# A selective-scan network on one core: the 3x3 convolution in 15 products of up to 128 rows, and the sums of chunks 0 and 1 copied out later

## The chip, the cores and the metric

The kernel runs on one core of a Trainium2 chip. The core has four compute engines, each with its own queue of instructions that it takes in order: TensorE (PE in the profile; its weight loads are PEld), VectorE (DVE), ScalarE (ACT) and GpSimd (POOL). SyncE (SP) issues the DMAs that this kernel uses, also in order. The metric is the device time of one execution in microseconds; smaller is better. Three runs of the kernel before took 5869.17, 5872.94 and 5878.88 us, so the median is 5872.94 us.

## The reference

The input is four images of 64 x 64 positions and 96 channels. Layer 0, which the change concerns, is group norm, then this (cut):

```python
xz = x @ W_in.T                      # 96 -> 384
xp, z = xz[..., :192], xz[..., 192:]
xc = silu(conv3x3(xp, conv_w) + conv_b)          # 192 -> 192 channels, zero padding
# four scans of 4096 positions: rows, columns, and both reversed
dts, Bs, Cs = split(x_proj_w @ xs)               # 6, 16 and 16 rows
delta = softplus(dt_proj_w @ dts + dt_proj_b)
h = exp(delta * A) * h + (delta * u) * B         # 16 states for each of 192 channels
y = sum(h * C, over states) + D * u
out = (sum of the four y) * silu(z) @ W_out.T
```

After it come a depthwise and a pointwise convolution with batch norm, linear attention with a feed-forward layer in 8-bit floats, and a filter by FFT over the 4096 positions with another such feed-forward layer.

## The kernel before, in words

**The head.** Image 0 goes through `before_scans` alone, ahead of all scans: `project` (load x, normalise, multiply with `w_in` to the 192 convolution inputs), `project_z`, `convolve`, `gates` and `scan_inputs`. An image is 8 blocks of 8 rows (512 positions). For each block and each half of 96 output channels, `convolve` adds up 18 products, 9 taps by 2 halves of 96 input channels. Its input `xp` has no padding, so a tap that would reach over the edge of the image writes a smaller window of the output (504, 448 or 441 columns in place of 512). Images 1 to 3 go through the same code beside the scans.

**The scans.** There are N = 192 phases: image, row or column order, and one of 24 groups of 8 channels; 8 channels by 16 states make 128 partitions. A phase has 4 chunks of 1024 positions. First come four forward steps, q = 0 to 3, then four reverse steps, k = 0 to 3 over chunks 3 to 0. This order is written by hand for all engines:

- ACT: `decay` (line 1458) writes exp(delta x A) of a chunk to PSUM (`pa`). The decays of chunks 1 and 0 are made a second time for the reverse steps, by `decay(n, 1, False)` at k = 1 and `decay(n, 0, True)` at k = 2; the next phase's first, `decay(n + 1, 0, True)`, is made at k = 3.
- DVE: the scan of a chunk (line 1700 forward, 1749 reverse), and the addition of the reverse scan to the forward one (line 1759). Once the convolutions are all done, chunk 0's reverse scan stays apart in its delta tile instead (`apart`), which spares that addition and costs POOL and PE one more operation each.
- POOL: `times_b` (line 1441) ahead of the scans, and `times_c` (1445, and `times_c_apart`, 1450) after them.
- PE: `reduce` (line 1472) adds the states up with a matrix of ones, in two halves of a phase (chunks 0 and 1, chunks 2 and 3), into one PSUM bank `py`. ACT copies it out (`result`, line 1480), and SP stores it in four DMAs (`store_result`, line 1489).
- SP: `load_delta` and `load_du` (both by way of line 1413) fetch a chunk for later phases, two DMAs each. Delta tiles have 5 buffers, `dl0` to `dl4`, which `place_of` gives out.

**Work beside the scans.** After each forward or reverse step, `pieces` puts in a piece of other work (images 1 to 3 up to their scans, turning of rows to columns, later layers of finished images), as far as each engine's credit goes: each piece names its cost by engine in `yield (PE, ACT, POOL, DVE, DMA)`, and a table gives credit by step. So costs in the code decide where a piece stands in the queues.

**The tail.** After the last phase, image 3 goes through the remaining layers alone.

Of the kernel before, what the change touches and what calls it, by code (L numbers as in the profile page):

```python
# [10 lines left out]
F32 = mybir.dt.float32  # L11
# [8 lines left out]
HW = 64  # L20
# [53 lines left out]
def layers(ctx: ExitStack, tc: tile.TileContext, a: dict, out):  # L74
# [110 lines left out]
    us, xps, xbs, szs = {}, {}, {}, {}  # L185
# [84 lines left out]
    def before_scans(b, wk, take, deep=1, prev=None):  # L270
# [3 lines left out]
        _, w_in, conv_w, xproj, dt_w = kept  # L274

        def count(stage):

            before = NBLK if prev is None else done[stage, prev]
            return done.get((stage, b), 0) + before - NBLK

        def project():
# [14 lines left out]
            for i in range(NBLK):  # L296
# [11 lines left out]
                xp = xps[b, i] = wk.tile([C, 2, RPB + 2, HW], F32, tag="xp", name="xp", bufs=2)  # L308
                for c in range(2):
                    for ra, rb in ((0, 5), (5, n)):  # L310
                        p, give = yield from take("p_xp", C, (rb - ra) * HW)
                        yield (0.8, 0, 0, 0)
                        nc.tensor.matmul(
                            p, lhsT=w_in[:, c * C : (c + 1) * C], rhs=xb[:, ra:rb, :],
                            start=True, stop=True,
                        )
                        yield NEXT
                        yield (0, 0.42, 0, 0)
                        nc.scalar.copy(xp[:, c, ra:rb, :], p.rearrange("p (r w) -> p r w", w=HW))
                        give()  # L320
# [26 lines left out]
        def convolve():  # L347
            for i in range(NBLK):
                yield from until(lambda: i < count("project"))
                r0, lo, hi = rows_of(i)  # L350
                xp = xps.pop((b, i))
                for oc in range(2):
                    p, give = yield from take("p_conv")
                    pr = p.rearrange("p (r w) -> p r w", w=HW)
                    todo = [(t, kc) for t in conv_taps() for kc in range(2)]
                    for k, ((ky, kx), kc) in enumerate(todo):
                        if k % 3 == 0:
                            yield (2.4, 0, 0, 0)
                        dy, dx, ra, rb, ca_, cb_ = tap_window(ky, kx, r0)
                        at = r0 + dy - lo  # L360
                        nc.tensor.matmul(  # L361
                            pr[:, ra:rb, ca_:cb_],
                            lhsT=conv_w[:, kc, ky * 3 + kx, oc * C : (oc + 1) * C],
                            rhs=xp[:, kc, at + ra : at + rb, ca_ + dx : cb_ + dx],
                            start=(k == 0), stop=(k == len(todo) - 1),
                        )
# [1002 lines left out]
    def last_place(name, k):  # L1369

        if (name, k) not in last_tiles:
            tags = {
                "w_in": [f"B{4 * (N % 2) + q}" for q in range(4)],
                "sz_in": [f"dl{place_of(*x)}" for x in ((N - 1, 3), (N - 1, 2), (N - 1, 1), (N, 0))],
# [30 lines left out]

    def channel_halves(t):

        return [t[k * 64 : k * 64 + 64, :] for k in range(2)]
# [6 lines left out]
    def load_delta(n, q):  # L1415
        if n < N:
            b, g, o = phases[n]
            t = dls[n, q] = big.tile([128, CH], F32, tag=f"dl{place_of(n, q)}", name="dl")
            load_channels(t, delta_s[o][b], g, q)
# [194 lines left out]
    for _ in group_norm(start.sbuf("start"), take, (0,), lambda: True):  # L1614
        pass
    start.close()
    kept += [
        const("w_in", [C, 2 * DI], a["w_inT"], wk),
        const("conv_w", [C, 2, 9, DI], a["convT"], wk),
# [47 lines left out]
    with tc.manual_schedule():  # L1667
        ordered[0] = True
        pas = [decay(0, 0, True), None, None, None]
        for n in range(N + 1):  # L1670
# [3 lines left out]
            for q in range(NCH):  # L1674
# [3 lines left out]
                else:  # L1678
                    load_delta(n + 1, 4 - q)
# [12 lines left out]
                else:  # L1692
                    times_b(n + 1, 0)
                    reduce(n - 1, 0, (0,))
# [12 lines left out]
            if end:  # L1707
                result(n - 1, 0)
# [13 lines left out]
            for k, q in enumerate(reversed(range(NCH))):  # L1722
# [4 lines left out]
                if k == 0:  # L1727
                    result(n - 1, 0)
                    load_delta(n + 1, 0)
                elif k == 1:  # L1730
                    store_result(n - 1, 0)
                    load_du(n + 2, 0)
                elif k == 2:
                    load_delta(n + 1, 3)
                else:
                    load_du(n + 2, 1)
# [4 lines left out]
                elif k == 2:  # L1741
                    pas[0] = decay(n, 0, True)
                elif k == 3:
# [43 lines left out]
def host_layout(i):  # L1787
# [7 lines left out]
    o["convT"] = f(w.transpose(2, 1, 3, 0))  # L1795
# [92 lines left out]
```

## Time and profile before

| | |
|---|---|
| median of three runs | 5872.94 us |
| profiled execution, its own time | 5867.99 us |
| its span | 5866.2 us |
| PE busy | 4369.5 us (74%) |
| DVE busy | 4801.4 us (82%) |
| ACT busy | 3018.7 us (51%) |
| POOL busy | 4413.7 us (75%) |
| moved by DMA | 1173 MB, 200 GB/s on average |
| granted TensorE clock, mean | 0.778 |

A line of the groups view names the line of the kernel, the engine, the operation, what it writes and reads with their shapes, and the count; behind the first bar stands busy time and the mean duration in ns, and behind the second the engine's idle time just before these instructions and what ended most of it. A line of the waits view reads "who waited <- for whom: us in total, times, longest". An fp32 product leaves two records in the trace. The record count of line 361, 2304, is so twice the 1152 products of the convolution.

### The profile page before, as it was taken

The numbers are of one execution on the slowest core, as the hardware profiler recorded it, in microseconds if no ns is written. First come the engines' busy times: TensorE is split into PE (matmuls) and PEld (weight loads), VectorE is DVE, ScalarE is ACT, GpSimd is POOL, SyncE is SP. The second block draws the span as 40 slices with busy tenths as digits, with TensorE's granted clock in tenths as the row PEclk, the third lists the DMA queues.
The fourth block names the chain that finished last, engine by engine and source line by source line (L and its number), as shares of the span: only waits on it lengthen the run. The fifth ranks groups of instructions, "written<-read, shape, count | busy, mean of one in ns | idle before, by whom it ended". The sixth has DMA issues, their size and how long they took to land. (4 is left out here: it accounts for less than half of the span.)

```text
span 5866.2 us, 64908 instructions
## 1 busy us (share of the span) xinstructions
PE 4369.5 (74%) x20038; PEld 1680.1 (29%) x20038; DVE 4801.4 (82%) x3479; ACT 3018.7 (51%) x4141; POOL 4413.7 (75%) x2118
## 2 busy tenths in 40 slices
PE   8978898799884776664566776667678667667888
PEld 3322222222220221142331221245222114333345
DVE  2049889889889888999889999999988999979364
ACT  4557666676555346645444546434444554424233
POOL 0258888789879778988778989888897898867200
PEclk9979889899886776666777876668678766767888
DMA  3258868887679878788988867679987578886003
GB/s 100 77 155 237 233 200 229 224 233 214 199 218 246 226 201 224 208 247 239 251 234 227 227 178 214 191 211 251 233 230 205 164 210 233 242 230 194 23 37 105
DMA packets 469417, 1173.13 MB, mean 200 GB/s; under 512 B 90496, under 2 KB 155628, under 8 KB 468972
## 3 DMA queue, kind: packets, MB, share of 16 engines
q1 hardware_dynamic: 469068, 1168.97, 72.5%
q8 instruction: 159, 2.61, 0.2%
q14 instruction: 190, 1.56, 0.1%
HBM read 1011.86 MB, written 156.76 MB: 199 GB/s over the span
## 5 line engine op out<-in xcount | busy, mean ns | idle before, releaser
L1445 POOL TENSOR_TENSOR S<-S,rep 128x1024 f32<-128x1024 f32 x768 | 1807.9, 2356 | 580.6 <-DVE S L1759 496.6
L1441 POOL TENSOR_TENSOR B<-B,rep 128x1024 f32<-128x1024 f32 x768 | 1798.3, 2357 | 107.8 <-DMA B<-du_s 67.8
L1458 ACT ACTIVATE pa<-dl,nega 128x1024 f32<-128x1024 f32 x1152 | 1283.9, 1116 | 1148.3 <-DVE S L1759 717.7
L1700 DVE TENSOR_TENSOR_SCAN S<-pa,S,B 128x1024 f32<-128x1024 f32 x576 | 1352.2, 2348 | 286.8 <-ACT pa L1458 117.2
L1472 PE MATMUL py<-S,red 128*32 128x512 f32 x3072 | 927.4, 845 | 667.2 <-POOL S L1445 456.8
L1749 DVE TENSOR_TENSOR_SCAN pa<-pa,edge,B 128x1024 f32<-128x1024 f32 x439 | 1032.1, 2351 | 67.9 <-ACT pa L1458 67.3
L361 PE MATMUL p_conv<-xp,conv_w 96*96 96x504 f32 (+3 forms) x2304 | 1054.4, 611 | 6.9 <-ACT u L374 4.9
L1759 DVE TENSOR_TENSOR S<-S,pa 128x1024 f32<-128x1024 f32 x631 | 764.7, 1212 | 1.9
L1700 DVE TENSOR_TENSOR_SCAN S<-pa,B 128x1024 f32<-128x1024 f32 x192 | 436.7, 2275 | 225.8 <-ACT pa L1458 179.9
L361 PEld LDWEIGHTS p_conv<-xp,conv_w 96*96 96x96 f32 x2304 | 382.2, 170 | 674.2 <-issue 636.5
L1480 ACT COPY ys<-py 128x512 f32<-128x512 f32 x384 | 222.8, 580 | 546.4 <-PE py L1472 487.3
L1749 DVE TENSOR_TENSOR_SCAN pa<-pa,B 128x1024 f32<-128x1024 f32 x192 | 440.9, 2296 | 5.4
L1472 PEld LDWEIGHTS py<-S,red 128*32 128x32 f32 x3072 | 111.8, 125 | 1148.0 <-POOL S L1445 647.4
L154 ACT COPY side<-side 96x256 f32<-96x256 f32 (+1 forms) x448 | 279.5, 628 | 127.8 <-DMA deltaT_s<-side 46.5
L1749 DVE TENSOR_TENSOR_SCAN dl<-pa,edge,B 128x1024 f32<-128x1024 f32 x137 | 320.7, 2341 | 14.6 <-ACT pa L1458 14.6
L1450 POOL TENSOR_TENSOR dl<-dl,rep 128x1024 f32<-128x1024 f32 x137 | 323.2, 2359 | 0.1
L1055 POOL CAST h<-y 128x1536 fp8e5<-128x1536 f16 x64 | 95.6, 1494 | 296.9 <-ACT y L766 273.6
L1472 PE MATMUL py<-dl,red 128*32 128x512 f32 x548 | 243.5, 752 | 30.3 <-POOL dl L1450 30.1
L877 PE MATMUL p_mean<-t,centre 96*96 96x512 f32 x256 | 172.6, 787 | 98.1 <-ACT sq L869 48.9
L527 PE MATMUL p_y<-side,ident 96*96 96x512 f32 x336 | 208.8, 771 | 24.3 <-DVE q L920 10.0
L833 PE MATMUL p_l<-x,taps 96*96 96x504 f32 (+3 forms) x432 | 202.3, 619 | 14.9 <-DMA x<-x 12.5
L458 POOL TENSOR_TENSOR r<-r,side 96x512 f32<-96x512 f32 x16 | 20.2, 1263 | 249.0 <-ACT side L443 248.8
(214 smaller groups left out, 5580.4 us busy)
## 6 DMA issues: line engine op xcount, KB each, us to landing
B<-du_s SPq DMA_DIRECT2D x768, 256.0 KB
dl<-delta_s SPq DMA_DIRECT2D x768, 256.0 KB
B<-duT_s SPq DMA_DIRECT2D x768, 256.0 KB
dl<-deltaT_s SPq DMA_DIRECT2D x768, 256.0 KB
z_s<-z SPq DMA_DIRECT2D x48, 512.0 KB
zl<-z_s SPq DMA_DIRECT2D x64, 384.0 KB
side<-y_s SPq DMA_DIRECT2D x120, 192.0 KB
rep<-bc_s SPq DMA_DIRECT2D x64, 256.0 KB
```

The costliest lines, as they stand in the source:

```text
L154: nc.scalar.copy(o.rearrange("p (w h) -> p w h", h=HW), t[:n, :].rearrange("p (h w) -> p w h", w=HW)[:, q * w : (q + 1) * w, :],)
L361: nc.tensor.matmul(pr[:, ra:rb, ca_:cb_], lhsT=conv_w[:, kc, ky * 3 + kx, oc * C : (oc + 1) * C], rhs=xp[:, kc, at + ra : at + rb, ca_ + d ...
L527: nc.tensor.matmul(p, lhsT=ident[:C, :C], rhs=x, start=(j == 0), stop=(j == 2))
L1441: nc.gpsimd.tensor_tensor(Bs[n, q], Bs[n, q], reps[n // NG, 0, q], ALU.mult)
L1445: nc.gpsimd.tensor_tensor(Ss[n, q], Ss[n, q], reps[n // NG, 1, q], ALU.mult)
L1450: nc.gpsimd.tensor_tensor(dls[n, 0], dls[n, 0], reps[n // NG, 1, 0], ALU.mult)
L1458: nc.scalar.activation(pa, dls[n, q], AF.Exp, scale=nega[:, g : g + 1])
L1472: nc.tensor.matmul(py[32 * j : 32 * j + 32, :], lhsT=red, rhs=x[:, k * BLK : (k + 1) * BLK], start=(i == 0), stop=(i == len(terms) - 1),)
L1480: nc.scalar.copy(ys, pys.pop((n, half)))
L1700: nc.vector.tensor_tensor_scan(s, pas[q], Bs[n, q], Ss[n, q - 1][:, CH - 1 : CH] if q else 0.0, ALU.mult, ALU.add,)
L1749: nc.vector.tensor_tensor_scan(to[:, ::-1], pas[q][:, ::-1], Bs[n, q][:, ::-1], edge if k else 0.0, ALU.mult, ALU.add,)
L1759: nc.vector.tensor_tensor(Ss[n, q], Ss[n, q], to, ALU.add)
```

## The change

There are two parts.

**The convolution.** The 192 input channels are split as 128 and 64. `low` holds the first 128, `high` the other 64 twice, the second copy one image row up, so that one product of 128 rows covers two taps of the upper 64 channels. Both have a column of zeros on each side and a row above and below, so every product has all 512 columns. For each block and half of the outputs that makes 9 products over `low`, 3 of 128 rows over `high` (tap rows 0 and 1), and 3 of 64 rows (tap row 2). The projection of the upper channels takes a weight `w_twice` that holds them twice; ACT copies its two halves out separately, so `project` has six copies a block and not four. The zero columns are set once for each of two pairs of tiles and each pool, the zero rows at the first and last block of each image. The weights are laid out anew on the host.

**The sums.** `reduce(n - 1, 0, (0,))` moves from q = 3 to k = 0. `result(n - 1, 0)` moves from k = 0 to k = 2, behind `decay(n, 0, True)`, and its store from k = 1 to k = 3. The loads of the next phase's delta change places in the queue: chunk 0 at q = 2 (before: k = 0), chunk 1 at q = 3 (as before), chunk 2 at k = 1 behind `load_du(n + 2, 0)` (before: q = 2), chunk 3 at k = 2 (as before). The buffers rotate so that a phase's chunk 0 goes where the phase before had chunk 2, chunk 1 where it had 3, chunk 3 where it had 1, and chunk 2 takes the spare one, which held chunk 0 of the phase before that.

The diff, cut to its core:

```diff
+        if id(wk) not in pads:
+            pads[id(wk)] = [
+                tuple(
+                    wk.tile([128, RPB + 2, HW + 2], F32, tag=f"{t}{k}", name=t)
+                    for t in ("low", "high")
+                )
+                for k in range(2)
+            ]
+            for t in (t for pair in pads[id(wk)] for t in pair):
+                for col in (0, HW + 1):
+                    nc.gpsimd.memset(t[:, :, col : col + 1], 0.0)
+        padded = pads[id(wk)]
...
-                xp = xps[b, i] = wk.tile([C, 2, RPB + 2, HW], F32, tag="xp", name="xp", bufs=2)
+                low, high = xps[b, i] = padded[i % 2]
+                if i == 0 or i == NBLK - 1:
+                    edge = 0 if i == 0 else RPB + 1
+                    nc.gpsimd.memset(low[:, edge, :], 0.0)
+                    nc.gpsimd.memset(high[:64, edge, :], 0.0)
+                at = lo - r0 + 1
                 for c in range(2):
                     for ra, rb in ((0, 5), (5, n)):
-                        p, give = yield from take("p_xp", C, (rb - ra) * HW)
+                        p, give = yield from take("p_xp", 128, (rb - ra) * HW)
                         yield (0.8, 0, 0, 0)
                         nc.tensor.matmul(
-                            p, lhsT=w_in[:, c * C : (c + 1) * C], rhs=xb[:, ra:rb, :],
+                            p, lhsT=w_twice if c else w_in[:, :128], rhs=xb[:, ra:rb, :],
                             start=True, stop=True,
                         )
                         yield NEXT
-                        yield (0, 0.42, 0, 0)
-                        nc.scalar.copy(xp[:, c, ra:rb, :], p.rearrange("p (r w) -> p r w", w=HW))
+                        yield (0, 0.84 if c else 0.42, 0, 0)
+                        rows = p.rearrange("p (r w) -> p r w", w=HW)
+                        if c == 0:
+                            nc.scalar.copy(low[:, at + ra : at + rb, 1 : HW + 1], rows)
+                        else:
+                            nc.scalar.copy(high[:64, at + ra : at + rb, 1 : HW + 1], rows[:64])
+                            ja, jb = max(at + ra - 1, 0), min(at + rb - 1, RPB)
+                            nc.scalar.copy(
+                                high[64:, ja:jb, 1 : HW + 1],
+                                rows[64:, ja + 1 - at - ra : jb + 1 - at - ra, :],
+                            )
...
-                    todo = [(t, kc) for t in conv_taps() for kc in range(2)]
-                    for k, ((ky, kx), kc) in enumerate(todo):
+                    for k in range(15):
                         if k % 3 == 0:
                             yield (2.4, 0, 0, 0)
...
+                        ky, kx = divmod(k, 3) if k < 9 else (2 * (k // 12), k % 3)
+                        src = low if k < 9 else high if k < 12 else high[:64]
                         nc.tensor.matmul(
...
+                            p, lhsT=conv_w[: src.shape[0], k, oc * C : (oc + 1) * C],
+                            rhs=src[:, ky : ky + RPB, kx : kx + HW],
+                            start=(k == 0), stop=(k == 14),
...
+    delta_places, spare = [(0, 1, 2, 3)], 4
+    while len(delta_places) <= N:
+        p = delta_places[-1]
+        delta_places.append((p[2], p[3], spare, p[1]))
+        spare = p[0]
...
-            t = dls[n, q] = big.tile([128, CH], F32, tag=f"dl{place_of(n, q)}", name="dl")
+            t = dls[n, q] = big.tile([128, CH], F32, tag=f"dl{delta_places[n][q]}", name="dl")
...
+    w_twice = wk.tile([C, 128], F32, tag="w_twice", name="w_twice")
+    for k in range(2):
+        nc.sync.dma_start(w_twice[:, k * 64 : k * 64 + 64], a["w_inT"][:, 128:DI])
     kept += [
         const("w_in", [C, 2 * DI], a["w_inT"], wk),
-        const("conv_w", [C, 2, 9, DI], a["convT"], wk),
+        w_twice,
+        const("conv_w", [128, 15, DI], a["convT"], wk),
...
                 if q < 2:
                     load_du(n + 1, q + 2)
                 else:
-                    load_delta(n + 1, 4 - q)
+                    load_delta(n + 1, q - 2)
...
                 else:
                     times_b(n + 1, 0)
-                    reduce(n - 1, 0, (0,))
...
             if end:
+                reduce(n - 1, 0, (0,))
                 result(n - 1, 0)
...
                 if k == 0:
-                    result(n - 1, 0)
-                    load_delta(n + 1, 0)
+                    reduce(n - 1, 0, (0,))
                 elif k == 1:
-                    store_result(n - 1, 0)
                     load_du(n + 2, 0)
+                    load_delta(n + 1, 2)
                 elif k == 2:
                     load_delta(n + 1, 3)
                 else:
+                    store_result(n - 1, 0)
                     load_du(n + 2, 1)
...
                 elif k == 2:
                     pas[0] = decay(n, 0, True)
+                    result(n - 1, 0)
```

## The prediction

> **What bounds the kernel now.** I read the busy table, then the windows view of the trace cut where the stages change, then the groups of instructions, the waits, and the timeline where a wait was large.
>
> The windows view; its columns are the stretch, busy time and instruction count of PE, PEld, DVE, ACT and POOL, the granted clock, the DMA share and GB/s:
>
> ```profile
> 0.00:20.00 20.00, 0.95 (x4) 0.79 (x4) 7.84 (x25) 2.99 (x4) 0.20 (x4) 1.00 0.68 182
> 27.00:329.00 302.00, 302.00 (x709) 114.46 (x708) 24.45 (x67) 164.82 (x221) 67.57 (x51) 0.97 0.30 87
> 359.00:1764.00 1405.00, 1217.39 (x3024) 380.87 (x3024) 1221.76 (x780) 907.78 (x1241) 1191.04 (x600) 0.87 0.79 220
> 1764.00:5421.00 3657.00, 2467.55 (x12945) 975.33 (x12945) 3332.56 (x2289) 1773.02 (x2394) 3077.98 (x1407) 0.72 0.81 220
> 5421.00:5866.20 445.20, 363.90 (x3327) 202.78 (x3323) 212.90 (x309) 139.75 (x238) 64.25 (x48) 0.84 0.18 58
> ```
>
> The head (image 0 ahead of its scans) is TensorE's: 302 of 302 us. From 359 to 5421 VectorE is the bound: 1221.8 of 1405 us while the convolutions of images 1 to 3 run beside the scans, 3332.6 of 3657 after that; it idles 183 + 324 us. The tail of 445 us is image 3's last layers.
>
> In the head, the timeline shows one half-block of the convolution, and the timeline in the scans two reduction products over 128 rows (each fp32 product is two records):
>
> ```profile
> 60.35 15.45 PE L361 MATMUL p_conv<-xp,conv_w 96*96 96x512 f32 x36
> 3002.48 1.92 PE L1472 MATMUL py<-S,red 128*32 128x512 f32 x4 [3.77 <-ACT ys L1480]
> ```
>
> 36 records in 15.45 us are 0.42 to 0.43 us each, back to back. Four 128-row records of 512 columns take 1.92 us, of which the last takes 0.62: again 0.43 apart.
>
> VectorE's idle time by step of a phase, from the groups (first forward scan; the other three; reverse scans that add into S; reverse scans of chunk 0 kept apart; idle time stands after the second bar):
>
> ```profile
> L1700 DVE TENSOR_TENSOR_SCAN S<-pa,B 128x1024 f32<-128x1024 f32 x192 | 436.7, 2275 | 225.8 <-ACT pa L1458 179.9
> L1700 DVE TENSOR_TENSOR_SCAN S<-pa,S,B 128x1024 f32<-128x1024 f32 x576 | 1352.2, 2348 | 286.8 <-ACT pa L1458 117.2
> L1749 DVE TENSOR_TENSOR_SCAN pa<-pa,edge,B 128x1024 f32<-128x1024 f32 x439 | 1032.1, 2351 | 67.9 <-ACT pa L1458 67.3
> L1749 DVE TENSOR_TENSOR_SCAN dl<-pa,edge,B 128x1024 f32<-128x1024 f32 x137 | 320.7, 2341 | 14.6 <-ACT pa L1458 14.6
> ```
>
> The very first scan's 170.6 us are the head's. There remain 55 us before first scans, 287 before the other forward ones, 82 before reverse ones. Most say that a decay (ACT, line 1458) came late. The waits say why:
>
> ```profile
> ACT ys L1480 <- PE py L1472: 487.3, 145, 9.7
> ACT pa L1458 <- DMA dl<-deltaT_s: 101.9, 22, 9.9
> ACT pa L1458 <- DMA dl<-delta_s: 80.7, 17, 11.0
> SPq L1413 <- PE py L1472: 182.5, 61, 10.2
> ```
>
> ACT stands 487 us at the copy of the sums, with decays behind it. SP stands 182 us at a delta load whose buffer the reduction still reads, so the decay of the next phase's chunk 0 starves. One case from the timeline:
>
> ```profile
> 5258.75 1.16 SPq L1413 DMA_DIRECT2D dl<-delta_s  x2
> ...
> 5264.35 2.15 ACT L1458 ACTIVATE pa<-dl,nega 128x1024 f32<-128x1024 f32 x2 [10.08 <-DMA dl<-delta_s]
> ...
> 5265.55 2.29 DVE L1700 TENSOR_TENSOR_SCAN S<-pa,B 128x1024 f32<-128x1024 f32 x1 [4.13 <-ACT pa L1458]
> ```
>
> A load issued 5.6 us before ACT can start, 10 us of idle ACT, 4.1 us of idle VectorE.
>
> **What the Trainium skill says.** "TensorE: Matmul & The Clock Gate", section LDWEIGHTS (loading the stationary operand): a weight load costs by its columns, not its rows; the section Back-to-back issue gap prices a product by its N alone. The trace agrees: 0.43 us a record with 96 rows and with 128. The same page, The HAM clock gate: an idle TensorE falls to half clock. The trace agrees in direction: 0.97 in the head at 100% busy, 0.72 after 1764 at 67%. "PSUM — Partial Sum Buffer", section Engine vs sequencer instructions: ScalarE's queue is strict FIFO. The trace agrees: decays sit out ACT's 487 us.
>
> **The convolution, in the head.** A middle half-block now takes 24 records of 504 columns at 0.42 and 12 of 512 at 0.427: 15.2 us; at the image's edge 14.7. The new one takes 30 x 0.427 = 12.8. Twelve middle and four edge half-blocks give 12 x 2.4 + 4 x 1.9 = **36 us off**, all on the path. Projections widen to 128 output rows at the same columns: 0. Two more ACT copies a block, 256 columns at 0.37 us (line 319's 256-column form): 8 x 0.74 = 5.9 us, covered by ACT's idle 137 of the 302 us; without that cover, 6 us. Pads: 12 memsets on POOL, which idles in the head: 0. The weights grow by 147 KB and w_twice adds 49 KB ahead of the first x block; the first 20 us are bandwidth-bound at 182 GB/s, so +1.1 us. Head: **-35** (bounds -37 and -22, the latter if ACT's answers come late at 32 us a block).
>
> **The convolution beside the scans.** 144 of 864 products fewer are some 125 us of TensorE off the path. What it gives is ACT waiting less for PE before decays; from the trace's records I trace 45 us of VectorE idle there to ACT behind p_dt, p_z, p_xp and p_conv. Against it 24 x 0.74 = 18 us more ACT copies ahead of decays. Bounds -25 and +15; I take -5. Twelve edge memsets on POOL, ten of which wait for products of the block two before, with times_b and times_c behind them: up to a step's three products, 2.6 us, for each of five pairs, but POOL idles 214 us of this stretch; 0, bound +13. The order of instructions shows this stage ending one phase sooner (138 reverse scans kept apart, not 137, each saving an add of 1.2 us): -1.
>
> **The copy of sums.** Reduction of chunk 0 goes from the fourth forward step to the first reverse step; its copy from there to the third reverse step, behind both recomputed decays. ACT's stall at line 1480 then no longer stands ahead of decay(n,1) and decay(n,0). Tracing late decays back, 43 us of the 82 us before reverse scans hang on it, nearly all before 1764. I take **-36**; bounds -50 and 0.
>
> **The delta loads.** Next phase's chunk 0 is now loaded at the third forward step into the place of this phase's chunk 2, five steps ahead of its decay and behind no reduction; only chunk 2 waits for the reduction, with four steps to spare. In 15 phases, with 42 of the 55 us before first scans, the decay had waited for its delta; I take **-36**. Chunk 3's load still stands behind a load that waits for the reduction, a step later than before, but no sooner needed: of about 25 us before the other forward scans, -10. Bounds for both -70 and 0.
>
> **New waits.** On PE the reduction no longer holds up the fourth step's side products (PE idles 166 us for POOL's dl there): a gain that I count as 0. On ACT the copy now has the sixth step's side work and decay(n+1,0) behind it; its reduction is by then two steps old. On SP the store at the last reverse step waits for that copy, with the load of du(n+2,1) behind; POOL needs that five steps later. On PE reduce(n,1) needs the bank that the copy frees; the copy ends about 1.7 us after the add that POOL's 2.35 us product must follow anyway. Together +13; bounds 0 and +150 (the rival below).
>
> **Sum.** Head -35, products in the scans -5, stage -1, copy -36, delta -46, new waits +13: -110. The tail's instruction counts on DVE, PE and POOL are unchanged: 0. The profiled execution took 5867.99 us (span 5866.2); 5868 - 110 = 5758. The median of the runs is 5 us above that execution, so **5763 us**.
>
> **Rivals.** *Only the head pays.* VectorE's freed time is taken back by POOL (84 to 85% busy) and DMA (80%): -35, and -15 of the rest, 5823. For it: POOL B and B loads already end some waits. Against: these total 50 us, and shortest phases run at 23.1 us, against 26.2 on average, with the same engines. *Everything pays*, with PE and ACT side work flowing better too: -35 - 50 - 55 - 10 = -150, 5723. *The copy becomes the wait, slower.* If the reduction runs as late relative to the copy's new turn as to the old one (487/145 = 3.4 us), decay(n+1,0), with some 6 us less 1.7 of ACT's own and 2.4 of side work, is late by 1.5 us in 145 phases: +218 against -123, about 5965. It decides from 0.64 us a phase (123/191). Against it: the copy moved two steps, the reduction one. *The products don't get cheaper*, if 128 rows cost more per column: then -75, 5798; the 128-row records speak against it.
>
> **How the numbers follow.** Forecast 0.58; head only 0.18; everything 0.13; copy becomes the wait 0.06; dearer products 0.03; unchanged 0.02. The measurement tells about 0.2% (12 us). Faster 0.58 + 0.18 + 0.13 + 0.03 = 0.92, of which I move 0.01 to slower for what I don't see. The range: the forecast's own is 5730 to 5795; it reaches down to 5715 and up to 5845 to take in the others but the slow one.
>
> **What would show it.** Right: head's scans start near 324 us, not 359; conv rows x1920 records at 0.43 us; SP's wait for py and ACT's wait for dl nearly gone; idle before first scans under 20 us beyond the head's; before reverse scans under 45. Wrong: ACT ys <- PE py as large as before, with decay(n+1,0) behind it; new waits for B on POOL; conv records longer than 0.43 apart at full clock.

## The result: faster by 0.4%, a quarter of the forecast

The kernel after takes 5847.7 us (median of six runs, 5835.47 to 5852.63); the kernel before, run beside it, 5872.95 us. The ratio is 0.9958, 95% interval 0.9945 to 0.9970: 25 us less, where 110 were forecast. The direction was right, the size wrong. The profiled execution took 5842.19 us, 26 us less than that of before, so the two traces hold the difference.

The windows view of the kernel after, cut where the stages change (columns as in the prediction; the last product of the convolutions starts at 1708.1 us, before at 1761.5):

```profile
27.00:290.00 263.00, 248.55 (x556) 89.93 (x555) 24.50 (x67) 156.03 (x218) 55.38 (x44) 0.95 0.29 84
347.20:1711.00 1363.80, 1131.62 (x2712) 335.70 (x2712) 1184.74 (x755) 910.61 (x1268) 1167.37 (x610) 0.85 0.79 220
1711.00:5389.00 3678.00, 2437.15 (x12967) 965.58 (x12968) 3363.72 (x2311) 1786.71 (x2414) 3100.86 (x1416) 0.73 0.82 222
5389.00:5840.40 451.40, 367.64 (x3329) 204.81 (x3328) 214.99 (x311) 140.87 (x240) 67.18 (x49) 0.83 0.17 57
```

Before, PE was busy 302 of 302 us in the head; now it idles 14 of 263. By the start of the first forward and of the last reverse scan: the head took 359.0 us and now 347.2 (-12, forecast -35); the scans 5059.5 and 5042.0 (-17, forecast -75); the tail 447.7 and 451.1 (+3, forecast 0).

The groups view of after, in the order in which the prediction shows them:

```profile
L1741 DVE TENSOR_TENSOR_SCAN S<-pa,B 128x1024 f32<-128x1024 f32 x192 | 436.4, 2273 | 189.5 <-ACT pa L1495 179.3
L1741 DVE TENSOR_TENSOR_SCAN S<-pa,S,B 128x1024 f32<-128x1024 f32 x576 | 1352.1, 2347 | 316.2 <-ACT pa L1495 128.6
L1792 DVE TENSOR_TENSOR_SCAN pa<-pa,edge,B 128x1024 f32<-128x1024 f32 x438 | 1029.7, 2351 | 46.3 <-ACT pa L1495 46.2
L1792 DVE TENSOR_TENSOR_SCAN dl<-pa,edge,B 128x1024 f32<-128x1024 f32 x138 | 323.1, 2341 | 16.3 <-ACT pa L1495 16.3
```

The very first scan's share for the head is 165.4 us, so 24 us are left before first scans (55 before), 63 before reverse scans (82 before), but 316 before the other forward ones (287 before). Idle time was taken from the places that the change aimed at, and more than half of it reappeared before other scans. The waits of after show that the aimed-at waits themselves are gone or small:

```profile
ACT ys L1517 <- PE py L1509: 18.2, 10, 2.8
ACT pa L1495 <- DMA dl<-delta_s: 72.0, 23, 11.2
ACT pa L1495 <- DMA dl<-deltaT_s: 56.1, 23, 7.8
```

ACT stood 487 us at the copy of the sums and stands 18; SP's 182 us at a load behind the reduction are 11. ACT's waits for delta went from 183 us only to 128.

### The profile page after: what moved, and what is told of

Read it like the earlier page. It is cut to its first block, busy times and chain, and to the rows that moved or that the text cites. A ratio compares the mean times of both kernels' runs of the same rounds, so it can differ in the third digit from the quotient of the medians.

```text
span 5840.4 us, 64640 instructions
## 1 busy us (share of the span) xinstructions
PE 4230.1 (72%) x19658; PEld 1612.3 (28%) x19658; DVE 4797.6 (82%) x3478; ACT 3044.6 (52%) x4205; POOL 4416.6 (76%) x2151
## 5 line engine op out<-in xcount | busy, mean ns | idle before, releaser
L1509 PE MATMUL py<-S,red 128*32 128x512 f32 x3072 | 905.5, 845 | 739.9 <-POOL S L1482 491.4
L390 PE MATMUL p_conv<-low,conv_w 128*96 128x512 f32 x1152 | 569.2, 647 | 8.7 <-ACT u L402 5.4
L390 PE MATMUL p_conv<-high,conv_w 128*96 128x512 f32 (+1 forms) x768 | 356.6, 602 | 0.0
L390 PEld LDWEIGHTS p_conv<-low,conv_w 128*96 128x96 f32 x1152 | 198.4, 179 | 390.8 <-issue 364.0
L1509 PE MATMUL py<-dl,red 128*32 128x512 f32 x552 | 219.2, 715 | 22.4 <-POOL dl L1487 22.3
```

Of the source, the lines that this page charges most:

```text
L390: nc.tensor.matmul(p, lhsT=conv_w[: src.shape[0], k, oc * C : (oc + 1) * C], rhs=src[:, ky : ky + RPB, kx : kx + HW], start=(k == 0), stop ...
L1509: nc.tensor.matmul(py[32 * j : 32 * j + 32, :], lhsT=red, rhs=x[:, k * BLK : (k + 1) * BLK], start=(i == 0), stop=(i == len(terms) - 1),)
```

## The experiments

All runs at a glance. "First scan" is when it starts in the profiled execution; "1 to 54" is the time from the first scan of phase 1 to that of phase 55 (the convolutions of images 1 to 3 run in the first 50 or so of them), "rest" from there to the first scan of phase 191; idle is VectorE's idle time just before scans in that stretch (the last few scans with the second), added up from the trace. Each ratio is to executions of the kernel before that ran beside that row; their medians lay between 5873 and 5881 us, so rows are best compared by their ratios.

| kernel | median, us | ratio to before (95%) | first scan | 1 to 54 | idle | rest | idle | tail |
|---|---|---|---|---|---|---|---|---|
| before | 5873 | 1 | 359 | 1446 | 170 | 3559 | 251 | 448 |
| after | 5847.7 | 0.9958 (0.9945 to 0.9970) | 347 | 1441 | 166 | 3546 | 233 | 451 |
| conv_only | 5860.2 | 0.9971 (0.9959 to 0.9983) | 349 | 1446 | 171 | 3561 | 250 | 448 |
| sums_only | 5854.6 | 0.9951 (0.9932 to 0.9971) | 361 | 1437 | 162 | 3549 | 238 | 450 |
| after_dvenorm | 5826.8 | 0.9910 (0.9895 to 0.9924) | 321 | 1448 | 173 | 3551 | 240 | 452 |
| before_dvenorm | 5874.1 | 0.9995 (0.9984 to 1.0006) | 356 | 1446 | 170 | 3572 | 255 | 447 |
| late_xr | 5862.3 | 0.9980 (0.9964 to 0.9995) | 345 | 1449 | 174 | 3483 | 209 | 525 |
| reduce_early | 5838.8 | 0.9932 (0.9910 to 0.9953) | 342 | 1435 | 161 | 3550 | 234 | 454 |
| loads_only | 5841.4 | 0.9941 (0.9919 to 0.9963) | 345 | 1443 | 168 | 3547 | 231 | 448 |
| no_second_copy | 5845.3 | 0.9943 (0.9920 to 0.9966) | 344 | 1431 | 156 | 3543 | 235 | 451 |
| before_no_copy | 5842.5 | 0.9944 (0.9922 to 0.9965) | 359 | 1416 | 141 | 3558 | 249 | 445 |
| delta_first | 5847.3 | 0.9948 (0.9928 to 0.9967) | 346 | 1450 | 175 | 3538 | 221 | 451 |
| less_pool | 5831.5 | 0.9921 (0.9896 to 0.9945) | 346 | 1446 | 171 | 3534 | 222 | 452 |
| early_dvenorm | 5824.6 | 0.9903 (0.9876 to 0.9930) | 326 | 1433 | 158 | 3539 | 229 | 448 |
| after_no_copy | 5837.2 | 0.9940 (0.9918 to 0.9962) | 347 | 1449 | 175 | 3531 | 229 | 445 |
| copy_k1 | 5848.0 | 0.9955 (0.9940 to 0.9971) | 347 | 1442 | 167 | 3545 | 232 | 451 |
| copy_k1_dvenorm | 5830.7 | 0.9924 (0.9905 to 0.9944) | 326 | 1439 | 164 | 3550 | 241 | 455 |
| answer_later | 5813.8 | 0.9891 (0.9866 to 0.9916) | 345 | 1425 | 150 | 3546 | 235 | 451 |
| answer_later_best | 5792.4 | 0.9862 (0.9841 to 0.9884) | 322 | 1422 | 147 | 3541 | 229 | 449 |
| before_later | 5870.8 | 0.9993 (0.9982 to 1.0004) | 357 | 1438 | 161 | 3554 | 239 | 445 |

Each of these stage figures is one execution. Kernels that are the same from the first scan on differ by up to 7 us in "1 to 54" (after 1441, after_dvenorm 1448) and 14 us in "rest" (before 3559, before_dvenorm 3572), and kernels with the same head have their first scan anywhere from 342 to 349 us; so a single figure tells some 10 us and no less.

**One part alone.** conv_only is the kernel before with the convolution's part of the diff, sums_only with the other part.

> Only the convolution's part of the change. Theory of the chain: in the head a block lasts one half-block of the convolution plus ACT's chain from the copy of u to the normalised next block, so only one of two half-blocks counts: the first scan starts at 346 to 349 us (359 before). Beside the scans, ACT still waits for PE as before and has 18 us more copies ahead of decays: phases 1 to 54 get 10 to 25 us longer. In all 5860 to 5880 us. Rival (convolution free beside the scans, sums worth little): 5850 to 5860.

> Only the sums' part of the change, with the delta loads. Theory: the waits before reverse scans and before first scans go as in the changed kernel, and what comes back before the other scans is partly the convolution's: scans 30 to 45 us shorter, head and tail as before, 5828 to 5845 us. Rival: the sums' part itself turns its gain into late loads of chunk 2 and into SP's wait at the later store; scans 10 to 20 us shorter, 5853 to 5863 us.

The convolution brought 10 us in the head and nothing beside the scans; the sums' part 14 us in the scans. Each falls short of its forecast by itself. Of the expectations, conv_only's was right in the head (349 us) and wrong beside the scans, where no time was lost (1446 us for 1446); sums_only came out within its rival's numbers. By these stages the parts make up the whole; by the ratios they take 17 and 29 us off and the whole only 25, which is a first sign, within the intervals no proof, that the parts get in each other's way.

**The head: who waits.** The timeline of before, from ACT's copy of a half-block's result (`u`) to the next normalised block, and then that of after:

```profile
212.75 0.68 ACT L374 ACTIVATE u<-p_conv,conv_b 96x512 f32<-96x512 f32 x1 [13.23 <-PE p_conv L361]
...
235.09 0.92 ACT L305 ACTIVATE xb<-xb,gn 96x640 f32<-96x640 f32 x1
236.93 0.70 PE L313 MATMUL p_xp<-xb,w_in 96*96 96x320 f32 x2
```

```profile
201.91 0.68 ACT L402 ACTIVATE u<-p_conv,conv_b 96x512 f32<-96x512 f32 x1 [8.34 <-PE p_conv L390]
...
209.33 7.89 PE L390 MATMUL p_conv<-low,conv_w 128*96 128x512 f32 x18
217.06 5.48 PE L390 MATMUL p_conv<-high,conv_w 128*96 128x512 f32 x12
224.69 0.92 ACT L320 ACTIVATE xb<-xb,gn 96x640 f32<-96x640 f32 x1
225.67 1.44 PE L333 MATMUL p_xp<-xb,w_in 96*128 96x320 f32 x2 [3.13 <-ACT xb L320]
```

A half-block now takes 13.2 us (30 records), close to the forecast's 12.8. But before, ACT's normalised block was done at 236.01, only 0.9 us before PE wanted it; from the copy of `u` to that point ACT had worked for 23.3 us without a gap. In the kernel after the same chain takes 23.7 us (201.91 to 225.61), PE is through sooner and waits 3.13 us. In the head PE waits so in five blocks:

```profile
PE p_xp L333 <- ACT xb L320: 14.4, 5, 3.4
```

The test moves this normalisation to VectorE, for image 0 alone, in the kernel after and in the kernel before:

```diff
-                nc.scalar.activation(
-                    xb[:, :n, :], xb[:, :n, :], AF.Identity, scale=gn[:, 0:1], bias=gn[:, 1:2]
-                )
+                if b == 0:
+                    nc.vector.tensor_scalar(
+                        xb[:, :n, :], xb[:, :n, :], gn[:, 0:1], gn[:, 1:2], ALU.mult, ALU.add
+                    )
+                else:
+                    nc.scalar.activation(
+                        xb[:, :n, :], xb[:, :n, :], AF.Identity, scale=gn[:, 0:1], bias=gn[:, 1:2]
+                    )
```

> The changed kernel with image 0's normalisation (head only) on VectorE, idle there, in place of ACT. Theory of the chain: it takes the normalisation out of ACT's queue, so PE need not wait for it, and the head becomes PE's again: first scan at 322 to 328 us (347.2 in the changed kernel), 5822 to 5828 us. Rival (128-row products or the granted clock cost the rest of the head's gain): first scan stays within 3 us of 347, 5843 to 5850 us.

> The kernel before with the same move of image 0's normalisation to VectorE. Theory: PE was busy throughout the head, with the normalisation landing 0.9 us before PE needs it, so nothing or little is won: first scan at 352 to 359 us, 5863 to 5873 us. Rival (ACT's chain alone sets the head already before): first scan 20 us or more earlier, 5853 us or less.

In the kernel after, the first scan comes at 321 us in place of 347 and the time falls by 21 us; in the kernel before, the same edit gives nothing. So ACT is what the head of the kernel after waits for, and PE was what the head of the kernel before waited for. By the last five blocks of the traces, a block's first projection came 40.2 to 42.3 us after that of the block ahead in the kernel before, 39.3 to 40.1 in the kernel after, and 34.4 to 36.1 in after_dvenorm. The windows view of after_dvenorm, to be held against the first line of after:

```profile
27.00:290.00 263.00, 263.00 (x608) 94.38 (x607) 28.04 (x73) 165.53 (x227) 66.76 (x53) 0.99 0.34 97
```

PE is busy all through again, at a granted clock of 0.99 and not 0.95. The Trainium skill ("TensorE: Matmul & The Clock Gate", The HAM clock gate) has an idle TensorE lose its clock. The trace agrees: behind the wait shown above the clock is at 0.50 (first line, after), and the projection's two products take 1.44 us, where they take 0.81 in after_dvenorm (second line), with no wait ahead of them:

```profile
225.60:229.00 3.40, 3.33 (x5) 1.63 (x6) 0.00 (x0) 1.67 (x4) 1.73 (x2) 0.50 0.53 168
209.40 0.81 PE L338 MATMUL p_xp<-xb,w_in 96*128 96x320 f32 x2
```

Waits are not all that costs clock, though: the kernel before has 0.96 in the stretch from 27 to 290 us without any.

**The convolution's extra copies.** no_second_copy leaves out the copy of the upper channels one row up, and with it those products' input, which stays zero.

```diff
-                            ja, jb = max(at + ra - 1, 0), min(at + rb - 1, RPB)
-                            nc.scalar.copy(
-                                high[64:, ja:jb, 1 : HW + 1],
-                                rows[64:, ja + 1 - at - ra : jb + 1 - at - ra, :],
-                            )
```

> The changed kernel without the second copy of the upper 64 channels (the shifted half of high stays zero, so three tap rows of those channels are left out of the convolution): 64 ACT copies of 0.37 us fewer, the same products. Theory: they stand in ACT's chain in the head, 0.74 us a block, 4 to 6 us in all, and ahead of decays beside the scans, where they cost 5 to 15 us; 5828 to 5840 us. Rival (hidden): 5842 to 5850 us.

The head starts its scans at 344 us, within what equal heads differ by, and the median is 2 us lower, as the rival said: the copies cost nothing that these runs can tell, in the head or beside the scans.

**Which piece of the sums' part.** loads_only has the kernel after with the reduction at q = 3, the copy at k = 0 and the store at k = 1, as before, so that only loads and buffers are new. reduce_early puts only the reduction back to q = 3.

> The changed kernel with reduction, copy and store of chunks 0 and 1 put back where they were; only the new places and order of the delta loads stay. Theory: the loads alone keep the gain before first scans (6 us there after phase 54, against 53 before), and the copy's move is worth little net since PE-bound stretches take it back: waits before the second reverse scans return to 50 us or more in phases 1 to 54, yet the whole is 5848 to 5858 us. Rival (the copy's move is worth what was forecast for it, some 30 us): 5865 to 5885 us.

> The changed kernel with the reduction of chunk 0 put back to the fourth forward step; copy, store and loads stay as changed. Rival (chunk 2's load stands behind the moved reduction): waits before the third forward scans after phase 54 fall from 65 to 45 us or less, 5828 to 5840 us. Theory of the queue: no difference beyond 6 us, 5842 to 5854 us, as PE's wait for POOL in the fourth step comes back.

loads_only is as fast as after, and faster than either case of its expectation: the loads' order carries all that the sums' part gives, and the moved copy and reduction, with nearly all of ACT's 487 us of waiting removed, carry nothing that these runs can tell. reduce_early's interval overlaps that of after, and third forward scans from phase 55 on still idle 60 us, not the 45 or less of its rival; whether its 9 us are real stays open.

**SP's queue.** Two runs ask what makes delta late after the change. In late_xr the residual's load, at which SP stood 113 us for a store to land, comes two steps later:

```diff
+            for _ in range(2 if i else 0):
+                yield NEXT
```

> The changed kernel; in the sums of finished images the load of the next block's input into the single residual tile is put two steps later, so that SP no longer stands at it until the store out of the same tile is through (113 us of SP waits, 28 times). Theory of the queue: SP, which takes its DMAs in order, keeps delta loads late in those phases, whatever the reduction does; ACT's waits for dl after phase 54 (115 us in the changed kernel) fall below 60 us and the scans get 12 to 30 us shorter, 5818 to 5836 us. Rival (loads are late because chunk 2's stands behind the moved reduction): waits for dl stay above 90 us, 5842 to 5850 us.

ACT's waits for delta fell from 128 to 77 us (after phase 54 from 115 to 66, where below 60 was expected), but later layers slid behind the scans (tail 525 us, with 4058 PE records for 3329), and the whole got slower than after. The run doesn't price SP's queue. delta_first changes only the order of two loads:

```diff
+                    load_delta(n + 1, 2)
                     load_du(n + 2, 0)
-                    load_delta(n + 1, 2)
```

> The kernel after, with the load of chunk 2's delta put ahead of the load of the product of delta and u at the second reverse step, so that it no longer stands behind the wait for a reverse scan (304 us over the execution). If the order of SP's queue is what makes chunk 2's delta late: ACT's waits for delta from phase 55 on fall from 115 us to below 50, the idle time before third forward scans from 65 to below 45, and the time to 5820 to 5832 us. If the lateness comes from the transfers themselves or is paid by the load that now comes second: waits for delta stay above 80 or POOL's waits for B grow from 93 us, and the time is within 8 us of 5848.

The time is that of after. By decay, added up from the traces for phases 55 on: before, the next phase's chunk 0 waited 127 us for its delta and chunk 3 44; after, chunk 0 nothing, chunk 1 5, chunk 2 56 and chunk 3 54; in delta_first chunk 2 19 and chunk 3 71, in all 104 for the 115 of after. So third forward scans idle less (39 us for 65), as the first theory asked, but waits for delta stay and the time with them, as the second said. Waits of after and then of delta_first (SP, from 1740 to 5391 us), which say why:

```profile
SPq L1450 <- DVE pa L1792: 210.5, 66, 6.4
```

```profile
SPq L1450 <- PE py L1509: 184.5, 52, 10.7
```

With the load of the product ahead, SP stands for a reverse scan that still reads `B`; with delta ahead, it stands for the reduction again, as in the kernel before. SP waits for something in either order, and what is queued behind is late: which chunk is late most, the order decides.

**Is POOL the bound?** The rival that only the head pays said so. less_pool leaves out POOL's product of C with chunk 2, 451 us of POOL:

```diff
-                if k > 0:
+                if k > 0 and k != 2:
                     times_c(n, q + 1)
```

> The kernel after, with POOL's product of C and the states of chunk 2 left out in every phase (192 products of 2.35 us, 451 us of POOL; the output lacks that factor). If POOL is what takes back VectorE's freed time (the reason of the rival that only the head pays): 60 us or more off the scans, so 5790 us or less. If the queues of ACT, SP and PE set VectorE's idle time: within 15 us of 5848, and idle time before scans falls by less than 20 of its 399 us.

The median is 16 us below that of after, one more than I had allowed the second theory, far from the 60 that the first asked for; the idle time before scans fell by 7 us of 399. POOL at 85% busy is not what takes VectorE's time back.

**What the copy is worth.** before_no_copy and after_no_copy leave ACT's copy of the first half's sums out and store zeros:

```diff
-        if n >= 0:
-            ys = yss[n, half] = big.tile([128, BLK], F32, tag="ys", name="ys", bufs=2)
+        if n >= 0 and half == 0:
+            if not blank:
+                blank.append(big.tile([128, BLK], F32, tag="blank", name="blank"))
+                nc.gpsimd.memset(blank[0], 0.0)
+            yss[n, half] = blank[0]
+            pys.pop((n, half))
+        elif n >= 0:
+            ys = yss[n, half] = big.tile([128, BLK], F32, tag="ys", name="ys", bufs=1)
             nc.scalar.copy(ys, pys.pop((n, half)))
```

> The kernel before, with the copy of the sums of chunks 0 and 1 left out on ACT (zeros are stored in their place, so that the stores stay; the output lacks these sums). It does more than the change can do for this copy: ACT neither stands at it nor spends its 0.58 us. My forecast held the copy's stall to be worth 36 us: then 5830 to 5840 us against 5873 to 5878, and VectorE's idle time before the third reverse scans of phases 1 to 54 falls from 54 to below 15 us with nothing taking its place. Rival, that ACT only goes on to the next wait, for products of the side work: 5855 to 5875 us; the wait for PE at the projection, the gate and the convolution grows by what the copy's wait gives up, and the sum of idle time before scans in phases 1 to 54 stays within 15 us of 170.

> The kernel after, with the copy of the sums of chunks 0 and 1 left out on ACT (zeros are stored; the output lacks these sums). Theory, the copy in its new place costs what it cost in the old one, because ACT has little slack left between the decay of chunk 0 and the next phase's first decay (10 us over phases 1 to 54): VectorE's idle time before scans in phases 1 to 54 falls from 166 us to 145 or less, phases 1 to 54 get 20 us shorter or more, and the time is 5815 to 5830 us. Rival, that the loads' new order or the later reduction took the gain back: idle time there stays within 10 us of 166, time within 8 us of 5848.

In the kernel before, phases 1 to 54 get 30 us shorter, VectorE's idle time before the third reverse scans there falls from 54 to 20 us, and nothing takes its place: the forecast's first case, against the rival. (The 347 us at the copy after 1764 us cost nothing: 3559 and 3558.) In the kernel after, leaving it out gives nothing in phases 1 to 54, 1449 for 1441, which refutes my theory there (the median, 10 us below that of after, lies a little outside the rival's 8). So the copy is free in its new place, and yet the 30 us were not earned. copy_k1 tries a third place, ahead of the decay for which ACT waits longest anyway, with the reduction at q = 3:

```diff
                 if k == 1:
+                    result(n - 1, 0)
                     pas[1] = decay(n, 1, False)
                 elif k == 2:
                     pas[0] = decay(n, 0, True)
-                    result(n - 1, 0)
```

> The kernel after, with the reduction of chunk 0 back at the fourth forward step and the copy of the sums at the second reverse step, right ahead of the recomputed decay of chunk 1, for which ACT waits for VectorE anyway (64 us over phases 1 to 54, 500 us after). If the copy's place is what took the gain back: idle time before scans in phases 1 to 54 falls to 150 us or less (steps one and two of the next phase back to some 35 us, third reverse step below 35), and the time is 5818 to 5832 us. If a copy in this place stands for the reduction again, as it did in the kernel before: third reverse step above 45 us, and the time is 5838 us or more.

> The same with image 0's normalisation on VectorE as well. If both gains stand: first scan near 322 us and 5795 to 5810 us. If the copy's place gives nothing, it is the kernel with both earlier edits again: 5818 us or more.

Nothing again: third reverse scans 47 us of idle time (25 in after), first and second forward scans 43 (65 in after). The sum stays, and my theory of the copy's place fell. What ACT waits for in this stage says more (from 359 to 1764 us with the old convolution, from 347 to 1798 with the new one; all convolutions lie inside). The kernel before, before_no_copy, after and after_no_copy:

```profile
ACT ys L1480 <- PE py L1472: 134.8, 41, 9.7
ACT xp L319 <- PE p_xp L313: 67.1, 31, 7.1
ACT u L374 <- PE p_conv L361: 43.6, 19, 5.0
```

```profile
ACT xp L319 <- PE p_xp L313: 77.7, 34, 6.7
ACT u L374 <- PE p_conv L361: 50.9, 22, 5.2
ACT sz L343 <- PE p_z L337: 49.1, 17, 7.3
```

```profile
ACT u L402 <- PE p_conv L390: 90.3, 22, 7.3
ACT low L341 <- PE p_xp L333: 62.4, 20, 6.7
ACT ys L1517 <- PE py L1509: 17.8, 8, 2.8
```

```profile
ACT u L402 <- PE p_conv L390: 94.6, 22, 7.8
ACT low L341 <- PE p_xp L333: 72.3, 20, 6.7
ACT sz L373 <- PE p_z L367: 39.7, 18, 5.9
```

Where the copy's wait goes and the convolution is the old one, the wait for the convolution hardly grows (44 to 51). In the kernel after it has doubled: ACT comes to copy `u` out while PE still works at it, up to 7.3 us, with decays behind. The test makes this copy one step later, in the kernel after, in the kernel with the lowest median so far (early_dvenorm: the reduction at q = 3 and the head's normalisation on VectorE), and in the kernel before:

```diff
-                    yield NEXT
+                    for _ in range(2 if b else 1):
+                        yield NEXT
                     yield (0, 0.68, 0, 0)
                     nc.scalar.activation(
                         u[:, oc, :], p, AF.Identity, bias=conv_b[:, oc : oc + 1]
```

> The kernel after with two edits at once: image 0's normalisation on VectorE, and the reduction of chunk 0 back at the fourth forward step. If both act in different stages, the head's 26 us (first scan near 321 us) and whatever the reduction gives (0 to 9 us) add: 5812 to 5828 us. If the head's gain were taken back in the scans, as happened to the kernel before: 5835 us or more.

> The kernel after, with ACT's copy of a half-block of the convolution of images 1 to 3 one step later than now, so that ACT no longer comes to it before PE is done. If these waits took the gain of the moved copy: ACT's waits for the convolution in phases 1 to 54 fall from 90 us to below 40, VectorE's idle time before scans there from 166 to 145 or less, and the time to 5820 to 5835 us. If ACT then stands as long at the next answer of PE (projection, gate), because PE is what paces this stage: its waits for PE in all stay within 20 of 238 us and the time within 8 us of 5848.

> The same together with image 0's normalisation on VectorE and the reduction of chunk 0 at the fourth forward step (5825 us without the later answer). If the later answer helps: 5797 to 5812 us. If not: 5817 us or more.

> The kernel before, with ACT's copy of a half-block of the convolution of images 1 to 3 one step later. If the waits for the convolution are new with the change (44 us in phases 1 to 54 here, 90 in the kernel after), there is little to take away while ACT stands at the copy of the sums: within 10 us of 5878. If they stood in the way before as well: 20 us or more less than 5878, as in the kernel after, and then they don't explain what became of the moved copy.

early_dvenorm, at 5825 us, shows that the head's gain stands. answer_later's median is 34 us below that of after; its profiled execution, the slowest of its four, is 18 us below, and 17 of these lie in phases 1 to 54, which last 1425 us with 150 of idle time. The waits of answer_later and then of before_later in that stretch:

```profile
ACT low L341 <- PE p_xp L333: 76.0, 24, 4.8
ACT sz L373 <- PE p_z L367: 64.8, 16, 9.6
ACT u L403 <- PE p_conv L390: 45.9, 19, 5.4
```

```profile
ACT ys L1481 <- PE py L1473: 167.4, 45, 10.7
ACT xp L319 <- PE p_xp L313: 71.6, 35, 3.4
ACT u L375 <- PE p_conv L361: 3.0, 4, 1.3
```

In the kernel before the same edit takes nearly all of the wait for the convolution away (44 to 3 us), ACT stands longer at the sums in exchange (135 to 167), idle time before third reverse scans rises from 54 to 73 us, and the time is the same within its interval. So what a wait of ACT costs depends on the others: before, taking the convolution's wait away earns nothing while ACT stands at the sums; after, where the sums' wait is gone and the convolution's has doubled, halving it earns time. My expectation for answer_later gave 40 us or less of the convolution's wait and 145 of idle time; both ended some 5 us above, while the time fell by more than I had said. ACT's waits for PE in all fell from 238 to 217 us, hardly more than the 20 that the rival allowed, as those for the projection and the gate grew. So where a wait stands seems to count, and not only how long it is; but the edit also shifts what follows in ACT's queue, and no run separates the two.

Two things stay open. The first is why the copy of `u` meets PE so much sooner in the kernel after. The waits of sums_only and of conv_only, from 359 to 1764 us:

```profile
ACT u L374 <- PE p_conv L361: 53.8, 20, 5.2
```

```profile
ACT u L402 <- PE p_conv L390: 62.2, 21, 7.3
```

Each part alone adds 10 to 19 us to the 44 of before, both together 47. That a piece of the convolution names the same cost to `pieces` as before, and a half-block has five pieces and not six, is a likely reason, only argued. The second is sums_only itself. It has the old convolution and nearly the old wait for it, and its third reverse scans in phases 1 to 54 idle 20 us, as in before_no_copy; yet its first and second forward scans idle 49 us there (31 before, 35 in before_no_copy), and it earns 9 us in these phases (1437), not 30 (1416). So the convolution's wait can't be all that took the copy's gain back.

answer_later_best, at 5792.4 us (ratio 0.9862), beats both kernels, and its own expectation: 81 us below before, by its ratio.

## Why the prediction was wrong

**The head, -35: -12.** The step that failed is "all on the path". PE did get cheaper as forecast: from first to last record the sixteen half-blocks took 257 us before and 221 after, 36 less. But each block is also a turn of ACT, from the copy of `u` to the next normalised block, and that chain (23.3 us in the block shown) came in only 0.9 to 3.8 us ahead of PE in the last five blocks of the kernel before. Beyond that PE waits, 14.4 us in all, and works at a lower clock behind each wait. My bound of -22 had this case, but with ACT's answers at 32 us a block, where blocks now come 39.3 us apart or more. The cover for the two new copies in ACT's idle 137 us didn't fail, as far as no_second_copy can tell. The 1.1 us for the larger weights are lost in the scatter, and the 182 GB/s that they were priced at is no ceiling: the scans move 220. after_dvenorm shows that the forecast was right about PE: with ACT's chain shortened the head is 38 us shorter than before.

**Products beside the scans, -5: 0** (1446 for 1446 in conv_only). Within the bounds. In conv_only the convolutions end 49 us sooner, at 1712 us, and phases 1 to 54 gain nothing by it. What I looked at, ACT less behind PE, went the other way: its wait for the convolution rose from 44 to 62, and to 90 in after.

**One phase sooner, -1:** as forecast, 138 reverse scans kept apart.

**The copy, -36: about 0.** The size of the stall was about right (30 us by before_no_copy, all of it in phases 1 to 54). The step that failed is that removing it earns it: there was no next wait in the sum. ACT's queue held one for the convolution, which the change made longer, from 44 to 90 us, and answer_later against before_later shows that it costs time only after the change. That it is not the whole reason, sums_only shows; the rest stays open. The bound of 0 covered the outcome; its reason was not seen.

**The delta loads, -46: about -13** (3559 to 3546). First scans of phases 55 on idle 6 us in place of 53, which is what was forecast of them. But "only chunk 2 waits for the reduction, with four steps to spare" and "chunk 3, -10" failed: both chunks are late (56 and 54 us from phase 55 on), third forward scans idle 65 us in place of 38, and delta_first moves most of the one's lateness to the other. Chunk 2's load hardly waits for the reduction now (SP stands 11 us for it); it waits behind a load that stands 211 us for a reverse scan, a wait that the sum had at nothing.

**New waits, +13.** SP does stand at the store of the copy, as said (148 us, from 1740 to 5391 us). None of this shows as a step of its own in the time.

**Rivals.** "Only the head pays" gave 5823 with the head at its full 35 and POOL as the reason; the head didn't pay fully and POOL isn't the reason. "The copy becomes the wait" named decay(n+1,0) behind the copy; first scans of phases 1 to 54 do idle 18 us in place of 2, but after_no_copy keeps these 18 us, so the copy isn't their cause. "The products don't get cheaper" is refuted by 30 records in 13.2 us. Of the signs that I had named for a right forecast, the price of the products and the end of SP's wait for the reduction came; but the head's scans start at 347 us and not 324, ACT still waits 128 us for delta, and first and reverse scans idle 24 and 63 us, not under 20 and 45. The range, 5715 to 5845, missed by 3 us: the head went past its bound of -22, and copy and loads came in near their bounds of 0 together, where the range had taken the poor ends one at a time.

## What to carry to other kernels

Ask of each stall in a queue what stands second: leave the stalled instruction out of the old kernel and out of the new one, and the two answers tell whether the stall was worth something and whether the change earned it. What a cheaper engine can earn is counted per turn of the loop, against the slack of the other chain that closes it, not against idle time over a stage: ACT idled 137 us of the head and had 0.9 to 3.8 us to spare in a block. And where one engine issues all loads in order, as here, look at what the new neighbours of a moved load wait for: here a third of the lateness went (172 us to 115) and the rest moved to other loads.

## What the runs showed of the hardware

Waits of TensorE of 1.8 to 3.4 us in the head cost more than their length: they add up to 14.4 us, and with them gone (after_dvenorm) the first scan came 26 us sooner. Behind the one at 222.5 us the granted clock was 0.50 for 3.4 us. In the nine traces in which PE is busy for at least 261 of the 263 us from 27 to 290, the clock there is 0.96 to 0.99; in the other eleven, with 6 to 15 us of waits, it is 0.93 to 0.95. The length of the waits doesn't order them (late_xr has 6 us and 0.93, after 14 us and 0.95).

The fp32 normalisation of 96x640 takes 0.60 us on VectorE and 0.92 on ScalarE, ahead of which ScalarE also loads a table for 1.28 us in most blocks of the head (at 223.40 us, ahead of the block shown); I had not counted that load as part of the chain. The head of the kernel after has 54 such loads, 69 us of ScalarE's time, and seven of them, 9 us, stand in the chain of 23.7 us shown.
